# Graph message passing on one core: comparison constants in PSUM, picks on four banks in five turns, and 80 chunks moved from picks to gathers

## The chip, the core and the metric

The kernel runs on one core of a Trainium2 chip. Its five engines are named as the profile names them: PE (TensorE, with PEld for its weight loads), DVE (VectorE), ACT (ScalarE), POOL (GpSimd) and SP (SyncE, which only issues transfers here). The metric is the device time of one execution in microseconds, as the median of the runs. SBUF is the on-chip memory that all engines read; PSUM is the smaller one, in eight banks of 512 float32 columns by 128 partitions, into which PE writes its results.

## The reference, cut to what matters

`x` holds 12500 nodes of 128 numbers. There are 400000 edges, sorted by their target `dst`, with a random source `src` and a random type 0 or 1.

```python
Xs = X[src]
m_data = Xs @ W_data.T + b_data
m_ctrl = Xs @ W_control.T + b_control
msg = jnp.where((edge_types == 0)[:, None], m_data, m_ctrl)
agg = jax.ops.segment_sum(msg, dst, num_segments=X.shape[0])
out = jax.nn.relu(agg + (X @ W_self.T + b_self))
result = layernorm(x + out)
```

The kernel turns this round: it first sums the source rows of each target, apart for the two types, then multiplies the sums by the weights. So its bulk is a sum of 400000 rows of `x`, each row found by a random index. Every float32 row is kept as three bfloat16 parts (`x3` in SBUF, `rows3` in DRAM, 3 x 128 columns), so that products with zeros and ones keep the float32 value.

## The kernel before

**Chunks, groups, sets.** The edges make 3125 chunks of 128, in `NG` = 25 groups of `GC` = 125 chunks. A group is cut into five stretches of 25 chunks: 5 "p" chunks and 20 "e" chunks. What is done with the 20 e chunks of a stretch is called a set here (`pairs` in the code). The function `sets(g)` says for how many of the five stretches the e chunks are a set: five where `g % EACH == 0`, else four. In a group of four sets the last stretch's 20 e chunks are handled as p chunks too. With `EACH = 3` there are 109 sets and 945 p chunks.

**P chunks: gathers.** For each p chunk POOL issues one indirect transfer (`msg<-rows,idx_g`, in `fetch`), which brings the 128 source rows from DRAM. DVE compares near targets with a running number (`psel<-near_col,near`, one instruction for 25 chunks), which gives a matrix of zeros and ones, and PE adds the rows with three products of 48 columns (`sums<-psel,msg`, in `add_rows`). `paced` ties each gather to a product of PE (its gate), so that gathers are spread over a set; `due` says from when a gather may go out, some 14 chunks ahead of its use. The pool `msg` holds 18 rows' tiles.

**E chunks: picks.** The sources of a set (2560 edges) are sorted into 100 cells (`NCELL`), a cell for the 128 nodes of one block of `x3`, with up to 32 places (`CAP`) each; what finds no place goes through a spare gather (`both<-rows,idx`, one for two sets). A long chain on DVE finds the places: `O<-cell_col,blk` (which cell), the `prod` instructions (how many of the cell come before), `rm<-rank_col,rank`, `rv`, and last `pick`, a matrix of zeros and ones for the 3200 places. A product with `pick` as weights picks the rows out of `x3`: four cells make 128 rows in 384 columns, and 25 such quads (`NQ`) make a set, the last one with two cells of its own and two that the spare gather fills. These products are `got<-x,pick`, weights of 32 columns each, four of them side by side in the array's four column groups. ACT copies `got` out of PSUM as bfloat16 (`emsg<-got`), DVE makes the matrices of the targets (`esel<-code_col,code`, three instructions for a set, of 10, 9 and 6 quads) and PE adds the rows up (`sums<-esel,emsg`, 172 columns).

**Turns.** A set's picks are made in five turns of `unit(t)` in `picked`: 5, 5, 5, 4 and 5 quads, and in the fourth the half quad too. In a turn `rows` is called twice: two quads into the tile `got2` (two PSUM banks), the others into `got3` (three banks), each followed by one copy on ACT; then `add` adds the rows of the turn before. A quad's 384 columns leave 128 of its bank unused. The eight banks are: five for `got`, two for `sums`, one for `side` (small results). Each `got` tile has one buffer, so a turn's picks wait for the copy of the turn before.

**Comparisons.** All zero-and-one matrices but `pick` and the small ones come from `select` (line 541 before): a DVE comparison of a constant table in SBUF (`cell_col`, `rank_col`, `code_col`, `near_col`) with a tile of codes in SBUF, both bfloat16, where the table is read again for each chunk or cell.

**Order.** The order of work on each engine is written out: `merged` sorts the pieces of a set by a fraction of the set (`chunks`, `units`, `order`, `more`), and the engines run what they get in that order. While set w is picked, the chain of set w + 2 and the beginning of set w + 3 run on DVE. When a group's last sums are in, `pass_on` and `finish` carry its edge over and make the output rows; before the change this was tied to the end of the group's last p stretch.

## Time and profile before

| | |
|---|---|
| time, median of 3 runs | 1671.41 us (1670.22 to 1672.55) |
| the profiled execution | 1674.53 us |
| its span, first to last instruction | 1672.8 us |
| granted TensorE clock, mean | 0.992 |
| DVE busy | 1566.8 us, 94% |
| PE busy | 1542.5 us, 92% |
| POOL busy | 1244.2 us, 74% |
| ACT busy | 1221.0 us, 73% |

Busy time is the union of an engine's instructions. On DVE and PE an instruction's recorded time overlaps the next one's, so that sums over groups come out higher than busy time. POOL's rows are the issuing of gathers; the idle time between two gathers stands apart from the busy time. In the chain of waits the time is put on the engine that released each step.

### The profile page before, as it was taken

The page shows a single profiled execution, that of the slowest core. Times are in us where ns is not written, and L with a number is a line of the kernel's source. Part 1 is how long each engine was busy: PE and PEld are TensorE (multiplying, and loading weights), DVE is VectorE, ACT ScalarE, POOL GpSimd, SP SyncE. Part 2 cuts the span into 40 slices and gives each one's busy share as a digit, 9 for nine tenths or more (in the row PEclk, how much of TensorE's full clock was granted, in tenths as well). Part 3 has the DMA queues.
Part 4 walks back from the last instruction along what each step waited for, and adds up shares of the span by engine and source line. Part 5 has one row for each costly group of instructions (what it writes and reads, how often), then busy time and mean ns, then how long its engine had stood idle before and what let it go on. Part 6 is the DMA issues. An engine that isn't in the chain of part 4 may idle for free.

```text
span 1672.8 us, 67687 instructions
## 1 busy us (share of the span) xinstructions
PE 1542.5 (92%) x27966; PEld 1218.8 (73%) x27966; DVE 1566.8 (94%) x4078; ACT 1221.0 (73%) x2056; POOL 1244.2 (74%) x1022
## 2 busy tenths in 40 slices
PE   1699999999999999999999999999999999999988
PEld 0477777777777777777777777777777777777766
DVE  9799998999999999999999999999999999999983
ACT  7677776777777778667777778677777777777764
POOL 1377777767787787888787887878787787888881
PEclk9899999999999999999999999999999999999999
DMA  7944444554455454444454445454545444554541
GB/s 223 283 142 136 143 139 134 154 148 141 142 156 145 147 155 133 150 140 143 149 156 139 148 142 152 139 159 135 158 124 164 147 144 131 157 152 126 151 124 33
DMA packets 147605, 246.05 MB, mean 147 GB/s; under 512 B 35565, under 2 KB 114264, under 8 KB 147288
## 3 DMA queue, kind: packets, MB, share of 16 engines
q1 hardware_dynamic: 99128, 142.50, 25.4%
q0 software_dynamic: 48160, 99.14, 22.8%
q8 instruction: 221, 3.62, 0.9%
q14 instruction: 96, 0.79, 0.1%
HBM read 224.04 MB, written 17.52 MB: 144 GB/s over the span
## 4 chain that ended last, share of the span: by engine, by line
DVE 57%; PE 25%; issue 7%; ACT 6%; DMA 3%; DVEq 2%; SPq 0%; POOL 0%; ACTq 0%; POOLq 0%
PE sums L803 11%; DVE esel L541 8%; PE got L997 7%; DVE prod L656 5%; DVE prod L648 5%; DVE pick L790 5%; DVE O L541 4%; DVE rv L713 3%; DVE prod L627 3%; ACT emsg L1011 3%; PE side L1118 2%; DVE psel L541 2%; DVE found L666 2%; DVE rm L541 2%; DVE prod L612 2%
## 5 line engine op out<-in xcount | busy, mean ns | idle before, releaser
L887 POOL DMA_INDIRECT msg<-rows,idx_g x945 | 1174.7, 1243 | 302.4 <-issue 124.3
L1011 ACT CAST emsg<-got 128x768 bf16<-128x768 f32 x1090 | 964.5, 930 | 302.9 <-PE got L997 287.7
L803 PE MATMUL sums<-esel,emsg 128*128 128x172 bf16 x7848 | 693.1, 238 | 7.3 <-DVE acc L876 4.1
L803 PEld LDWEIGHTS <-emsg 128*128 128x128 bf16 x7848 | 570.8, 98 | 115.1 <-issue 104.2
L997 PE MATMUL got<-x,pick 128*32 128x384 bf16 x10682 | 561.7, 330 | 13.5 <-ACT emsg L1011 5.4
L997 PEld LDWEIGHTS <-pick 128*32 128x32 bf16 x10682 | 242.3, 96 | 140.0 <-issue 19.9
L541 DVE TENSOR_TENSOR esel<-code_col,code 128x1720 bf16<-128x1720 bf16 x327 | 292.8, 896 | 6.4 <-PE sums L803 6.3
L803 PE MATMUL sums<-psel,msg 128*128 128x48 bf16 x2835 | 162.6, 184 | 5.2 <-DVE acc L876 4.7
L803 PEld LDWEIGHTS <-msg 128*128 128x128 bf16 x2835 | 134.9, 97 | 14.1 <-issue 11.9
L656 DVE TENSOR_TENSOR prod<-prod 128x1200 bf16<-128x1200 bf16 x218 | 136.3, 625 | 5.5 <-DVE prod L648 1.2
L648 DVE TENSOR_TENSOR prod<-O,ahead 128x2000 bf16<-128x2000 bf16 x109 | 130.7, 1199 | 2.7
L541 DVE TENSOR_TENSOR O<-cell_col,blk 128x2000 bf16<-128x2000 bf16 x109 | 129.8, 1191 | 0.5 <-ACT blk L443 0.5
L963 POOL DMA_INDIRECT both<-rows,idx x55 | 64.4, 1171 | 70.0 <-DMA srcs<-in_src_dram 25.8
L726 PE MATMUL side<-rv,O 128*128 128x64 bf16 x2180 | 84.8, 195 | 32.9 <-DVE rv L713 32.0
L790 DVE TENSOR_SCALAR pick<-pick,lane_f 128x3200 bf16<-128x3200 bf16 x109 | 112.7, 1034 | 2.4 <-DMA pick<-there 2.4
L726 PEld LDWEIGHTS <-O 128*128 128x128 bf16 x2180 | 80.1, 100 | 43.0 <-DVE rv L713 24.8
L541 DVE TENSOR_TENSOR psel<-near_col,near 128x1200 bf16<-128x1200 bf16 x125 | 95.9, 767 | 0.0
L627 DVE TENSOR_TENSOR prod<-prod 128x500 bf16<-128x500 bf16 x327 | 94.3, 288 | 0.4
L713 DVE TENSOR_TENSOR rv<-rm,vals 128x1280 bf16<-128x1280 bf16 x109 | 89.4, 820 | 0.0
L622 DVE TENSOR_TENSOR prod<-O 128x1000 bf16<-128x1000 bf16 x109 | 73.9, 678 | 2.1 <-DVE bits L701 0.3
L876 DVE TENSOR_TENSOR acc<-acc,sums 128x172 f32 (+2 forms) x234 | 65.5, 280 | 6.3 <-PE sums L803 6.2
L642 DVE TENSOR_REDUCE ahead<-side 128x100 bf16<-128x200 f32 x109 | 39.2, 360 | 34.2 <-PE side L634 33.6
(197 smaller groups left out, 1522.4 us busy)
## 6 DMA issues: line engine op xcount, KB each, us to landing
pick<-there SPq DMA_DIRECT2D x108, 800.0 KB
msg<-rows,idx_g POOLq DMA_INDIRECT x945
acc<-acc_start SPq DMA_DIRECT2D x23, 640.0 KB
rows<-x SPq DMA_DIRECT2D x6, 1344.0 KB
xs<-in_x_dram SPq DMA_DIRECT2D x99, 62.5 KB
out_dram<-h SPq DMA_DIRECT2D x99, 62.5 KB
xt<-in_x_dram SPq DMA_DIRECT2D x6, 896.0 KB
cnt<-cnt_start SPq DMA_DIRECT2D x22, 160.0 KB
```

Source lines behind the costliest of these rows:

```text
L541: ins = nc.vector.tensor_tensor(sel.rearrange("p n (w t) -> p n w t", t=2), col[:rows].rearrange("p (o w t) -> p o w t", o=1, t=2).to_broa ...
L622: return nc.vector.tensor_add(h[:, :2 * CQ], s["O"][:, :2 * CQ], s["O"][:, 2 * CQ:])
L627: return nc.vector.tensor_add(h[:, to:to + n], h[:, a:a + n], h[:, b:b + n])
L648: return nc.vector.tensor_tensor(s["prod"][:, :, :NCELL], s["O"], s["ahead_b"].rearrange("p (o j) -> p o j", o=1).to_broadcast([P, EC, NCE ...
L656: return nc.vector.tensor_add(prod[:, :, :h], prod[:, :, :h], prod[:, :, h:2 * h])
L713: placed[:] = [nc.vector.tensor_tensor(rv.rearrange("p c v (r t) -> p c v r t", t=2), s["rm"].rearrange("p c (o r t) -> p c o r t", o=1, t ...
L726: nc.tensor.matmul(s["rk"][:m, :2 * CAP], s["held"][:, c * NCELL:c * NCELL + m], s["rv"][:, c].rearrange("p v r -> p (v r)"), start=(c == ...
L790: return nc.vector.tensor_scalar(t, t, lane_f, None, op0=OP.is_equal)
L803: last = nc.tensor.matmul(out, msg[:, j * D:(j + 1) * D], sel, start=(start and j == 0), stop=stop, skip_group_check=True)
L887: return nc.gpsimd.indirect_dma_start(out=msg, out_offset=None, in_=rows3[:, :], in_offset=bass.IndirectOffsetOnAxis(ap=codes["p", g][0][: ...
L997: last = behind(last, lambda: nc.tensor.matmul(ps[CAP * a:CAP * (a + 1), :], slots[w]["pick"][:, a * NQ + q, :], x3[:, 4 * q + a - a0].rea ...
L1011: s["out"] = nc.scalar.copy(msg[:, :n], ps[:, :n, :3 * D])
```

## The change

Three things are changed together.

**Constants in PSUM.** After the tables are built, `on_psum` copies each of them, two bfloat16 as one float32 word, into the tile `cols`, which takes one PSUM bank (250 of its 512 columns are used), and hands back a bfloat16 view of it. `select` is the same; its first input now lies in PSUM. This is five small copies at the start.

**Picks on four banks.** `got2` and `got3` become `got0` and `got1`, two banks each. The first two quads of a turn go to `got0`, the last two to `got1`. In a turn of five, the middle one is picked in its three parts of 128 columns, which go to the free ends of the banks: parts 0 and 1 in `got0`, part 2 in `got1`. So a quad of this kind is 12 products of 128 columns in place of 4 of 384. In the fourth turn the half quad is split in the same way. Over the kernel the picks go from 10682 products to 14070. ACT copies 1024 and 896 columns in place of 768 and 1152, and in the fourth turn the half quad takes two small copies in place of one.

**80 chunks.** `EACH` goes from 3 to 6: five groups in place of nine have five sets. So there are 105 sets and 1025 p chunks. To this belong: `paced` is called for a second gate in turns 1 and 3 (before: in turn 2), so 12 times a set; and the end of a group is now found as the later of its last p stretch and its last set (`ended`).

```diff
--- before.py
+++ after.py
@@ -32,7 +32,7 @@
 NE = 5
 NWIN = 2 * NE
 LAG = 2
-EACH = 3
+EACH = 6
 DPC = P * N // E
 PAD = 10
 PW = DPC + 2 * PAD
@@ -218,6 +218,7 @@
     ps1 = ctx.enter_context(tc.tile_pool(name="ps1", bufs=1, space=PSUM))
     ps2 = ctx.enter_context(tc.tile_pool(name="ps2", bufs=2, space=PSUM))
     psg = ctx.enter_context(tc.tile_pool(name="psg", bufs=1, space=PSUM))
+    psc = ctx.enter_context(tc.tile_pool(name="psc", bufs=1, space=PSUM))
 
     def side():
 
@@ -351,6 +352,18 @@
     rank_col = table(CAP, 0, "rank_col")
     code_col = table(2 * EW, 1, "code_col")
     near_col = table(2 * PW, 0, "near_col")
+    cols = psc.tile([P, 512], FP, name="cols")
+
+    def on_psum(t):
+        n = t.shape[1] // 2
+        at = cols[:, used[0]:used[0] + n]
+        used[0] += n
+        nc.vector.tensor_copy(at, t.bitcast(FP))
+        return at.bitcast(BF)
+
+    used = [0]
+    cell_cols = [on_psum(t) for t in cell_cols]
+    rank_col, code_col, near_col = on_psum(rank_col), on_psum(code_col), on_psum(near_col)
     ident_b = keep.tile([P, P], BF, name="ident_b")
     nc.vector.tensor_copy(ident_b, ident)
     lane_f = keep.tile([P, 1], FP, name="lane_f")
@@ -801,7 +814,7 @@
     def add_rows(out, msg, sel, start, stop):
         for j in range(3):
             last = nc.tensor.matmul(
-                out, msg[:, j * D:(j + 1) * D], sel, start=(start and j == 0), stop=stop, skip_group_check=True
+                out, msg[j], sel, start=(start and j == 0), stop=stop, skip_group_check=True
             )
         return last
 
@@ -940,7 +953,7 @@
             sel = s["sel"][:, c].rearrange("p (t w) -> p t w", t=2)
             at = DPC * c
             rows = cells_of(s["ps"], AW, 0).rearrange("p (t w) -> p t w", t=2)[:, :, at:at + PW]
-            add_rows(rows, s["msg"], sel, c == 0, c == n - 1)
+            add_rows(rows, [s["msg"][:, j * D:(j + 1) * D] for j in range(3)], sel, c == 0, c == n - 1)
             if c == 0:
                 counts.append(s)
             elif c == n - 1 and s in counts:
@@ -992,25 +1005,37 @@
             with after(first), tc.high_priority():
                 return f()
 
-        def pick(ps, q, a0=0, a1=4, last=None):
+        def pick(out, q, a0=0, a1=4, part=slice(None), last=None):
             for a in range(a0, a1):
                 last = behind(last, lambda: nc.tensor.matmul(
-                    ps[CAP * a:CAP * (a + 1), :], slots[w]["pick"][:, a * NQ + q, :],
-                    x3[:, 4 * q + a - a0].rearrange("p j d -> p (j d)"), start=True, stop=True, skip_group_check=True,
+                    out[CAP * a:CAP * (a + 1), :], slots[w]["pick"][:, a * NQ + q, :],
+                    x3[:, 4 * q + a - a0, part].rearrange("p j d -> p (j d)"),
+                    start=True, stop=True, skip_group_check=True,
                 ))
             return last
 
-        def rows(q, n, room, half=False):
-            ps = psg.tile([P, room, 512], FP, name=f"got{room}")
-            msg = two.tile([P, room, 3 * D], BF, name=f"emsg{room}")
-            for k in range(n):
-                last = pick(ps[:, k, :3 * D], q + k, last=last if k else None)
-                s["msg"][q + k] = msg[:, k, :]
+        def rows(q, n, k, half=False):
+
+            ps = psg.tile([P, 2, 512], FP, name=f"got{k}")
+            msg = two.tile([P, 2, 512], BF, name=f"emsg{k}")
+            shared = NQ - 1 if half else q + 2
+            first, last = (q, None) if k == 0 else (q + n - 2, None)
+            parts = (0, 1) if k == 0 else (2,)
+            for j in range(2):
+                last = pick(ps[:, j, :3 * D], first + j, last=last)
+                s["msg"][first + j] = [msg[:, j, d * D:(d + 1) * D] for d in range(3)]
+            for j, d in enumerate(parts):
+                ends = (lead, lead + 2) if half else (0, 4)
+                last = pick(ps[:, j, 3 * D:], shared, *ends, slice(d, d + 1), last)
+                if not half:
+                    s["msg"].setdefault(shared, []).append(msg[:, j, 3 * D:])
             if half:
-                last = pick(ps[:, n, :3 * D], NQ - 1, lead, lead + 2, last)
-            s["out"] = nc.scalar.copy(msg[:, :n], ps[:, :n, :3 * D])
-            if half:
-                nc.scalar.copy(s["msg"][NQ - 1][half_rows, :], ps[half_rows, n, :3 * D])
+                s["out"] = nc.scalar.copy(msg[:, :, :3 * D], ps[:, :, :3 * D])
+                to = s["last"][half_rows, parts[0] * D:(parts[-1] + 1) * D]
+                nc.scalar.copy(to.rearrange("p (k d) -> p k d", d=D), ps[half_rows, :len(parts), 3 * D:])
+            else:
+                width = 1024 if k == 0 else 512 + 3 * D
+                s["out"] = nc.scalar.copy(*(t.rearrange("p k d -> p (k d)")[:, :width] for t in (msg, ps)))
             return last
 
         def add(q0, q1):
@@ -1026,11 +1051,13 @@
                 assert not spare
                 if "both" in slots[w]:
                     slots[w]["last"] = two.tile([P, 3 * D], BF, name="last", bufs=1)
-                s["msg"][NQ - 1] = slots[w]["last"]
-            paced(w + (t + 0.5) / turns, rows(bounds[t], 2, 2))
+                s["last"] = slots[w]["last"]
+                s["msg"][NQ - 1] = [s["last"][:, d * D:(d + 1) * D] for d in range(3)]
+            n = bounds[t + 1] - bounds[t]
+            paced(w + (t + 0.5) / turns, rows(bounds[t], n, 0, t == 3))
             if t == 1 and w > 0 and w % 2 == 0:
                 spare.append(lambda: spare_rows(w))
-            gate = rows(bounds[t] + 2, bounds[t + 1] - bounds[t] - 2, 3, t == 3)
+            gate = rows(bounds[t], n, 1, t == 3)
             if t == 0:
                 choose(0, 10)
                 gates = ending() or [gate]
@@ -1044,7 +1071,7 @@
             if t > 0:
                 gates = add(bounds[t - 1], bounds[t])
             paced(w + (t + 1) / turns, gates[0])
-            if t == 2:
+            if t in (1, 3):
                 paced(w + (t + 1) / turns, gates[-1])
             for u in tiled.get(t, []):
                 u()
@@ -1237,6 +1264,10 @@
             due.append(at)
             n += 1
         closed.setdefault(int(at), []).append(p)
+    ended = {}
+    for g in range(NG):
+        last_p = next(w for w, ps in closed.items() if g * NE + NE - 1 in ps)
+        ended.setdefault(max(last_p, each_e.index((g, sets(g) - 1))), []).append(g)
 
     due[:] = [(LAG - 0.1) * (k + 0.5) / AHEAD for k in range(AHEAD)] + due[:-AHEAD]
 
@@ -1313,14 +1344,13 @@
         )
         slots.pop(w)
         rest = []
-        for p in closed.pop(w, []):
-            gp, ip = divmod(p, NE)
-            if ip == NE - 1:
-                rest.append(lambda gp=gp: pass_on(gp))
-                if gp < NG - 1:
-                    rest += finish(gp, range(4))
-                if gp + 2 < NG:
-                    rest.append(lambda gp=gp: begin_acc(gp + 2))
+        closed.pop(w, None)
+        for gp in ended.pop(w, []):
+            rest.append(lambda gp=gp: pass_on(gp))
+            if gp < NG - 1:
+                rest += finish(gp, range(4))
+            if gp + 2 < NG:
+                rest.append(lambda gp=gp: begin_acc(gp + 2))
     ending()
     for u in rest + last:
         u()
```

What the change does to the order of instructions is shown at three places.

DVE, the middle of the program, around the comparison for a set's last six quads (1032 columns; `prod`, `rm` and `rv` belong to the set two further on). Before:

```order
L656 TENSOR_TENSOR prod<-prod 128x20x60
L541 TENSOR_TENSOR esel<-code_col,code 128x1032
L656 TENSOR_TENSOR prod<-prod 128x20x30
L661 TENSOR_TENSOR prod<-prod 128x20x14
L666 TENSOR_REDUCE found<-prod 128x20
L612 TENSOR_TENSOR prod<-blk_21792,blk_184 128x20x20
L671 CAST rank<-found 128x40
L541 TENSOR_TENSOR rm<-rank_col,rank 128x640
L678 SCALAR_TENSOR_TENSOR key<-rank,pk 128x20
L541 TENSOR_TENSOR esel<-code_col,code 128x1720
```

and now:

```order
L669 TENSOR_TENSOR prod<-prod 128x20x60
L554 TENSOR_TENSOR esel<-cols,code 128x1032
L669 TENSOR_TENSOR prod<-prod 128x20x30
L674 TENSOR_TENSOR prod<-prod 128x20x14
L679 TENSOR_REDUCE found<-prod 128x20
L625 TENSOR_TENSOR prod<-blk_23265,blk_193 128x20x20
L684 CAST rank<-found 128x40
L554 TENSOR_TENSOR rm<-cols,rank 128x640
L691 SCALAR_TENSOR_TENSOR key<-rank,pk 128x20
L554 TENSOR_TENSOR psel<-cols,near_20978 128x1200
L726 TENSOR_TENSOR rv<-rm,vals_22769 128x1280
```

The instructions are the same, of the same shapes and nearly in the same order; what moved is that `esel`, `rm`, `psel` and `O` read `cols` in place of four tables.

POOL, the middle of the program; `both` is the spare gather that comes once in two sets. Before:

```order
L887 DMA msg<-rows_105,idx_g 128x384 x18
L963 DMA both<-rows_105,idx 128x384
L887 DMA msg<-rows_105,idx_g 128x384 x18
L963 DMA both<-rows_105,idx 128x384
L887 DMA msg<-rows_105,idx_g 128x384 x17
```

and now:

```order
L900 DMA msg<-rows_108,idx_g 128x384 x20
L976 DMA both<-rows_108,idx 128x384
L900 DMA msg<-rows_108,idx_g 128x384 x20
L976 DMA both<-rows_108,idx 128x384
L900 DMA msg<-rows_108,idx_g 128x384 x21
```

There were 17 or 18 gathers for two sets in this stretch, and now there are 20 or 21.

ACT, two turns of a set around the half quad (the fourth turn); 1024 and 896 or 768 and 1152 are columns. Before:

```order
L1011 CAST emsg_22288<-got_22287 128x768
L1011 CAST emsg_22301<-got_22300 128x1152
L1011 CAST emsg_22393<-got_22392 128x768
L1011 CAST emsg_22404<-got_22403 128x768
L1013 CAST last<-got_22403 64x384
L1011 CAST emsg_22469<-got_22468 128x768
L1011 CAST emsg_22482<-got_22481 128x1152
```

and now:

```order
L1038 CAST emsg_23359<-got_23358 128x1024
L1038 CAST emsg_23380<-got_23379 128x896
L1033 CAST emsg_23467<-got_23466 128x2x384
L1035 CAST both<-got_23466 64x256
L1033 CAST emsg_23485<-got_23484 128x2x384
L1035 CAST both<-got_23484 64x128
L1038 CAST emsg_23522<-got_23521 128x1024
L1038 CAST emsg_23543<-got_23542 128x896
```

The columns copied for a turn of five quads are 1920 as before, split otherwise, and the half quad has one more copy.

## The prediction

> **What bounds the kernel now.** I read the page's busy shares first, then the table of stretches, the chain, and the groups of POOL.
>
> ```profile
> PE 1542.5 (92%) x27966; PEld 1218.8 (73%) x27966; DVE 1566.8 (94%) x4078; ACT 1221.0 (73%) x2056; POOL 1244.2 (74%) x1022
> 800.00:1200.00 400.00, 383.56 (x7081) 306.43 (x7080) 385.39 (x981) 296.91 (x508) 318.35 (x260) 1.00 0.50 148
> DVE 57%; PE 25%; issue 7%; ACT 6%; DMA 3%; DVEq 2%; SPq 0%; POOL 0%; ACTq 0%; POOLq 0%
> L642 DVE TENSOR_REDUCE ahead<-side 128x100 bf16<-128x200 f32 x109 | 39.2, 360 | 34.2 <-PE side L634 33.6
> L726 PE MATMUL side<-rv,O 128*128 128x64 bf16 x2180 | 84.8, 195 | 32.9 <-DVE rv L713 32.0
> ```
>
> In 400 us of the middle DVE is busy for 385.39 and PE (first number) for 383.56: 96% both, at full clock. The chain runs on DVE for 57% and on PE for 25%, and the largest wait that DVE has for PE is 33.6 us in all, the largest of PE for DVE 32.0. So both are full, DVE a little more, and a cut counts only if both get it.
>
> POOL looks like the engine with room, at 74%. Its groups say otherwise:
>
> ```profile
> L887 POOL DMA_INDIRECT msg<-rows,idx_g x945 | 1174.7, 1243 | 302.4 <-issue 124.3 <-PE got L997 72.5 <-PE sums L803 64.0
> L963 POOL DMA_INDIRECT both<-rows,idx x55 | 64.4, 1171 | 70.0 <-DMA srcs<-in_src_dram 25.8 <-ACT emsg L1011 21.5 <-ACT idx L591 13.9
> L887 POOL DMA_INDIRECT msg<-rows,idx_g x945: 945/1122/4102, 66.8 to 1636.2; - x189
> ```
>
> A gather takes 1.243 us and 302.4 / 945 = 0.32 us stand before it, 1.563 together; 1000 gathers of both kinds make some 1560 us, and the first starts at 66.8, the last at 1636.2, 1569 us. POOL issues one gather behind the other all the time. It is full too, although nobody waits for it yet: the list of PE's waits has none for `msg`. And a gather can be as short as 0.945 us, so 0.298 us of the mean is something that holds it up. A stretch of POOL's and DVE's timelines shows what:
>
> ```profile
> 1041.27 0.94 POOL L887 DMA_INDIRECT msg<-rows,idx_g  x1 [0.30 <-issue]
> 1042.52 1.18 POOL L887 DMA_INDIRECT msg<-rows,idx_g  x1 [0.30 <-PE got L997]
> 1044.00 0.99 POOL L887 DMA_INDIRECT msg<-rows,idx_g  x1 [0.31 <-issue]
> ...
> 1041.17 0.39 DVE L876 TENSOR_TENSOR acc<-acc,sums 128x240 f32 x1
> 1041.48 0.25 DVE L627 TENSOR_TENSOR prod<-prod 128x200 bf16<-128x200 bf16 x1
> ...
> 1041.92 0.95 DVE L541 TENSOR_TENSOR esel<-code_col,code 128x1548 bf16<-128x1548 bf16 x1
> 1043.73 0.43 DVE L839 TENSOR_TENSOR acc<-acc 128x280 f32<-128x280 f32 x1
> ```
>
> The second gather starts inside `esel`, which ends at 1042.87, and the gather ends 0.83 us after that; the third starts inside line 839, which ends at 1044.16, and ends 0.83 us after that. Both DVE instructions read two tiles in SBUF. The first gather starts inside `acc<-acc,sums`, whose second input lies in PSUM, and is not held up. So a gather that begins under a DVE instruction with two SBUF inputs waits for that instruction's end, and one with an input in PSUM lets it pass.
>
> **The change part by part.** *Four sets fewer, on DVE.* The groups by shape, x109 once a set (busy us, mean ns):
>
> ```profile
> L648 DVE TENSOR_TENSOR prod<-O,ahead 128x2000 bf16<-128x2000 bf16 x109 | 130.7, 1199 | 2.7
> L541 DVE TENSOR_TENSOR O<-cell_col,blk 128x2000 bf16<-128x2000 bf16 x109 | 129.8, 1191 | 0.5 <-ACT blk L443 0.5
> L541 DVE TENSOR_TENSOR esel<-code_col,code 128x1720 bf16<-128x1720 bf16 x109 | 113.9, 1045 | 6.0 <-PE sums L803 5.9
> L790 DVE TENSOR_SCALAR pick<-pick,lane_f 128x3200 bf16<-128x3200 bf16 x109 | 112.7, 1034 | 2.4 <-DMA pick<-there 2.4
> L541 DVE TENSOR_TENSOR esel<-code_col,code 128x1548 bf16<-128x1548 bf16 x109 | 103.8, 953 | 0.4 <-PE sums L803 0.4
> L541 DVE TENSOR_TENSOR psel<-near_col,near 128x1200 bf16<-128x1200 bf16 x125 | 95.9, 767 | 0.0
> L713 DVE TENSOR_TENSOR rv<-rm,vals 128x1280 bf16<-128x1280 bf16 x109 | 89.4, 820 | 0.0
> L656 DVE TENSOR_TENSOR prod<-prod 128x1200 bf16<-128x1200 bf16 x109 | 85.6, 786 | 5.5 <-DVE prod L648 1.2 <-DVE acc L876 0.7
> L541 DVE TENSOR_TENSOR esel<-code_col,code 128x1032 bf16<-128x1032 bf16 x109 | 75.0, 688 | 0.0
> L622 DVE TENSOR_TENSOR prod<-O 128x1000 bf16<-128x1000 bf16 x109 | 73.9, 678 | 2.1 <-DVE bits L701 0.3 <-issue 0.3
> L541 DVE TENSOR_TENSOR rm<-rank_col,rank 128x640 bf16<-128x640 bf16 x109 | 53.2, 488 | 2.6
> L666 DVE TENSOR_REDUCE found<-prod 128x20 f32<-128x320 bf16 x109 | 52.2, 479 | 1.1
> ...
> L678 DVE SCALAR_TENSOR_TENSOR key<-rank,pk 128x20 f32<-128x20 bf16 x109 | 18.7, 171 | 0.0
> L876 DVE TENSOR_TENSOR acc<-acc,sums 128x172 f32 x109 | 35.3, 324 | 6.2 <-PE sums L803 6.2
> ```
>
> The large ones (without `psel`, which stays at 125) sum to 968 us, twelve smaller x109 groups from `found` 52.2 to `key` 18.7 to 402, and the spare slots' small ones to 71: 1441 / 109 = 13.2 us a set. Most records overlap the next by 0.08 us (in the timeline above 1041.17 + 0.39 against 1041.48), and a set has 26 of them: 13.2 - 2.1 = 11.1 us. Four sets: **-44 us on DVE**. The 80 chunks add nothing here, as `psel` already covers 25 chunks wherever it stands.
>
> *Four sets fewer and 80 chunks more, on PE.* From the chain in a stretch where PE leads (start, us, what):
>
> ```profile
> 828.07 0.93 PE got L997 x20
> 829.21 1.27 PE sums L803 x21
> 837.54 0.60 PE side L726 x20
> 838.14 0.15 PE sums L803 x6
> 855.25 0.26 PE sums L918 x12
> ```
>
> Six products of `msg` take 0.15 us, 0.025 each; 15 of `esel` the rest of 1.27, 0.075 each; 20 of `got` 0.93. A set has 98 of `got` (4.56 us), 72 + 3 of `esel` (5.6), 20 of line 726 (0.60) and about 0.6 us of small ones: 11.3, four sets -45 us. The chunks add 240 products of `msg`, +6 us. **-39 us on PE**.
>
> *The quad in three pieces.* No row has 128 columns on four column groups. Bounds: five quads of 384 columns take 0.93, 0.186 each; if 3 x 128 columns run as 384 do, the pieces cost nothing. `L918` is the nearest row, 12 products of 96 to 120 columns on two column groups in 0.26 us: six pairs, 0.043 a pair, 0.055 for 128 columns. If the pieces too ran only two at a time, 12 of them would take 6 x 0.055 = 0.33 in place of 0.186, +0.145 in each of four turns a set (in the half quad's turn two run side by side before and after): +61 us on PE over 105 sets. I take 0.01 a turn, +5 us, since `got` runs four groups side by side and `L918` shows that short products with loads between them keep their pace. PE then has -34.
>
> *ACT.* As many columns; one copy more a set:
>
> ```profile
> L1011 ACT CAST emsg<-got 128x768 bf16<-128x768 f32 x654 | 512.7, 802 | 300.5 <-PE got L997 286.5 <-ACT emsg L1011 3.7 <-PE sums L803 3.0
> L1011 ACT CAST emsg<-got 128x1152 bf16<-128x1152 f32 x436 | 489.6, 1123 | 2.4 <-PE got L997 1.3 <-PE side L747 0.2
> ```
>
> 384 columns more cost 0.32, so the fixed part of a copy is some 0.16 us: +17 us, in front of which ACT idles for 300 us waiting for PE. Hidden there; without that idle time it would cost those 17.
>
> *The constants: DVE's rate.* The 650 comparisons that are left (five a set, and 125 of `psel`) run at two elements a nanosecond now: from `rm` to `O`, 1360 columns cost 703 ns, 0.52 each, and 0.15 is fixed. No row has a two-byte input in PSUM. Float32 in PSUM is no dearer than in SBUF: line 839's group (both in SBUF) takes 0.43 for 280 in the rows above, `acc` with an input in PSUM 0.324 for 172, and between the two lie 1.0 ns a column. So the fixed part is the same, and the float32 pace is that of its type in both memories. Bounds: nothing, or one element a cycle as float32 has, +0.52 ns a column (the first rival). A gain I exclude, since it is POOL that waits for DVE and not DVE for POOL: an instruction with two SBUF inputs takes the same time whatever POOL does, as the spread of `rv` shows (shortest, median, longest):
>
> ```profile
> L713 DVE TENSOR_TENSOR rv<-rm,vals x109: 803/824/827, 28.2 to 1619.2; 128x1280 bf16<-128x1280 bf16 x109
> ```
>
> I take nothing. Five copies at the start, of few columns: +1.
>
> *The constants: POOL's time.* A gather that begins anywhere in an instruction of length L waits L/2 on average, so the delay goes with the sum of L squared over a set. The comparisons have `O` 1.42, `esel` 1.09 + 0.91 + 0.47, `rm` 0.24, `psel` 0.59 x 125/109: 4.8. What still holds the port has `prod` of `ahead` 1.44, `pick` 1.07, `rv` 0.67, 0.62, 0.46 and small ones 0.75: 5.0. So 0.298 goes to 0.15 and a gather to 1.10 us, bounds 0.945 and 1.243. There will be 1025 + 53 = 1078 gathers: 1078 x (1.10 + 0.32) = 1531, from 66.8, and behind the last one 1672.8 - 1636.2 = 37: POOL alone ends at 1635. With the 0.30 of the rows above in place of 0.32 it is 1613.
>
> *Sum.* Against the profiled execution's 1674.5: DVE -44, PE -34; weighted by their shares of the chain (57 and 25) -41, +1 for the start, +2 since POOL is as full as before: 1636.5. The profiled execution lies 3.1 above the median 1671.4; so 1633.
>
> **Rivals.** *One element a cycle (slower).* If a two-byte input in PSUM halves the rate, `O` grows by 1.04, `esel` by 2.24, `rm` by 0.33, 3.61 x 105 = 379, and `psel` by 0.62 x 125 = 78: 457 us on the engine that leads: 2090. It turns the sign from a tenth of that price on (41 us). For it: PSUM rows here all run at one a cycle. Against: they are all float32, and so does float32 in SBUF. [...]
>
> *POOL becomes the bound (slower).* If PSUM inputs of these comparisons held gathers up as before, 1078 x 1.563 + 104 = 1789, 1786 by the median. It decides from a mean gather of about 1.15 us, where POOL alone would end at the old time; the rows of 1041.27 speak against it.
>
> *Pieces two at a time (slower).* PE -39 + 61 = +22: 1693. It decides from some +35 on, where PE no longer gains.
>
> [...]
>
> *Twice the gain.* DVE and PE wait for one another for 33.6 and 32.0 us; with evenly sized `got` tiles and gathers that land earlier half of that may go: 1603.
>
> **Chances.** Forecast 0.66, one element a cycle 0.10, POOL 0.06, pieces 0.04, dearer start 0.05, twice the gain 0.09. The likeliest one's own range is 1612 to 1655: PE's -34 alone or less at the top, DVE's whole -44 and some waits at the bottom. Extended to the twice-gain and the no-change case it is 1602 to 1673, which leaves 0.20 out, all of it above. About 0.2% (3 us) is what can be told from no change. Faster: 0.66 + 0.09 = 0.75. Same: 0.05. Slower: 0.20.
>
> **What would show it.** `O<-cols` at 1.19 us and `esel` at 0.69 to 1.05, as now: no loss of rate; at 2.2 us the first rival. Gathers' mean near 1.10, with many of 0.945 that begin under `esel` or `O`: the port is free; idle time before them over 0.30 says that POOL now waits for its gates. 28 products of `got` in 0.95 us or so: pieces run four wide. DVE's busy time falls to some 1523 and PE's to 1508, each still 96% of the middle. Wrong I am if the time falls much less while both busy times fall as said: then POOL's gathers are late, and PE has waits for `msg`.

## The result, and the profile after

The changed kernel took 1648.41 us (median of 4 runs, 1645.56 to 1649.66), the kernel before on the same chip 1670.82 us (1670.08 to 1672.55): a ratio of 0.9865, with a 95% interval from 0.9852 to 0.9877. That is 22.4 us less, where 38 were forecast. The profiled execution took 1648.49 us; the forecast for it was 1636.5. One thing is needed to read the times further down: beside the runs whose labels begin with e, f and h the kernel before takes 1948 to 1983 us in place of 1671, and in the traces of these runs PE halts without a recorded reason.

The changed kernel's page (first its span, then the busy times, then the chain), and one row of its table of stretches:

```profile
span 1646.4 us, 74069 instructions
PE 1514.0 (92%) x31152; PEld 1247.6 (76%) x31152; DVE 1542.1 (94%) x3979; ACT 1200.0 (73%) x2097; POOL 1157.8 (70%) x1100
DVE 53%; PE 28%; issue 8%; ACT 7%; DMA 2%; DVEq 2%; POOL 0%; SPq 0%; ACTq 0%; POOLq 0%
500.00:900.00 400.00, 383.71 (x7971) 319.34 (x7969) 386.29 (x995) 296.60 (x526) 303.07 (x281) 1.00 0.52 153
```

DVE is busy for 24.7 us less than before, PE for 28.5 us less, and both still fill 96% of the middle. The gain is there, and it is smaller on both engines than said. DVE's groups by shape:

```profile
L554 DVE TENSOR_TENSOR O<-cols,blk 128x2000 bf16<-128x2000 bf16 x105 | 125.0, 1190 | 0.5 <-ACT blk L456 0.5
L554 DVE TENSOR_TENSOR esel<-cols,code 128x1720 bf16<-128x1720 bf16 x105 | 109.0, 1038 | 0.9 <-PE sums L816 0.9
L554 DVE TENSOR_TENSOR psel<-cols,near 128x1200 bf16<-128x1200 bf16 x125 | 96.0, 768 | 0.3 <-issue 0.3
L554 DVE TENSOR_TENSOR rm<-cols,rank 128x640 bf16<-128x640 bf16 x105 | 51.5, 490 | 3.3
L679 DVE TENSOR_REDUCE found<-prod 128x20 f32<-128x320 bf16 x105 | 50.8, 484 | 3.1
L684 DVE CAST rank<-found 128x40 bf16<-128x40 f32 x105 | 28.7, 274 | 0.0
```

The five comparisons cost what they cost from SBUF (`O` 1190 ns against 1191, `esel` 1038 against 1045). One row has become dearer, and the change doesn't touch it: `rank`, a copy of 40 columns from SBUF to SBUF, takes 274 ns. It took 180 before:

```profile
L671 DVE CAST rank<-found 128x40 bf16<-128x40 f32 x109 | 19.7, 180 | 0.0
```

POOL's groups, and the spread of the gathers (shortest, median, longest, then the first and the last start):

```profile
L900 POOL DMA_INDIRECT msg<-rows,idx_g x1025 | 1091.4, 1065 | 360.7 <-issue 142.6 <-PE got L1010 95.5 <-PE sums L816 83.4
L900 POOL DMA_INDIRECT msg<-rows,idx_g x1025: 940/946/2039, 68.9 to 1613.6; - x171
```

The median gather is now one that nothing holds up, 946 ns where it was 1122, and the idle time before a gather is 0.35 us where it was 0.32: POOL now waits for its gates. ACT's copies take 1012 and 911 ns, together as much as the 802 and 1123 before, behind an idle time for PE's picks:

```profile
L1038 ACT CAST emsg<-got 128x1024 bf16<-128x1024 f32 x420 | 425.0, 1012 | 176.6 <-PE got L1010 160.9 <-issue 3.1 <-ACT both L1035 2.5
L1038 ACT CAST emsg<-got 128x896 bf16<-128x896 f32 x420 | 382.6, 911 | 14.0 <-PE got L1010 13.0 <-PE side L760 0.3 <-issue 0.2
```

And the picks of two turns of five quads, in the chain of a stretch where PE leads:

```profile
849.27 0.93 PE got L1010 x28
851.74 0.93 PE got L1010 x28
```

28 products, 16 of 384 columns and 12 of 128, take the 0.93 us that 20 of 384 took.

**Where DVE's missing 20 us are.** Two things were found in the two traces. The first is `rank`. The rows of POOL and DVE around one of them (start, us, then what):

```profile
1058.82 0.95 POOL L900 DMA_INDIRECT msg<-rows,idx_g  x1 [0.30 <-issue]
...
1058.62 0.49 DVE L679 TENSOR_REDUCE found<-prod 128x20 f32<-128x320 bf16 x1
1059.14 0.38 DVE L625 TENSOR_TENSOR prod<-blk,blk 128x400 bf16<-128x400 bf16 x1
1059.44 0.34 DVE L684 CAST rank<-found 128x40 bf16<-128x40 f32 x1
1059.81 0.49 DVE L554 TENSOR_TENSOR rm<-cols,rank 128x640 bf16<-128x640 bf16 x1
```

The gather runs from 1058.82 to 1059.77. `rank` starts inside it and ends at 1059.78, with the gather's end. The `prod` of line 625, which starts 0.3 us earlier, isn't held. In 89 of the 105 sets `rank` starts during a gather. In 63 of them it starts 0.53 to 0.77 us into one, that is in its last 0.2 to 0.4 us, and ends with it; in the other 26 it takes at most 191 ns. In all it costs 9.8 us more than 105 copies of 180 ns would. Before the change `rank` started during a gather too, in 74 of 109 sets, but ended with one in only 3: what changed is the point of the gather at which it starts.

The second is the order. The scheduler placed `esel` (1720 columns) between `found` and the `prod` that `found` needs in 43 of 109 sets before, and in none of 105 now; `found` stood right behind that `prod` in 33 sets and stands there in 91 now. In both traces an instruction that needs the result of the one right before it starts 34 ns after its end; one that doesn't starts some 83 ns ahead of it. Counted over all of DVE's records, gaps of 30 to 40 ns went from 467 to 561 (562 in g_after, the same kernel again). Each costs 0.117 us, of which the 0.083 of lost overlap shows in DVE's busy time: 94 of them are 11 us, 8 of it busy time.

### The profile page after: what moved, and what is told of

Its sections match the earlier page's. It is cut to its first block, busy times and chain, and to the rows that moved or that the text cites. A ratio compares the mean times of both kernels' runs of the same rounds, so it can differ in the third digit from the quotient of the medians.

```text
span 1646.4 us, 74069 instructions
## 1 busy us (share of the span) xinstructions
PE 1514.0 (92%) x31152; PEld 1247.6 (76%) x31152; DVE 1542.1 (94%) x3979; ACT 1200.0 (73%) x2097; POOL 1157.8 (70%) x1100
## 4 chain that ended last, share of the span: by engine, by line
DVE 53%; PE 28%; issue 8%; ACT 7%; DMA 2%; DVEq 2%; POOL 0%; SPq 0%; ACTq 0%; POOLq 0%
PE sums L816 12%; PE got L1010 8%; DVE esel L554 7%; DVE prod L669 5%; DVE prod L661 5%; DVE O L554 4%; DVE pick L803 4%; PE side L1145 3%; DVE prod L640 3%; DVE rv L726 3%; DVE prod L635 3%; DVE rm L554 2%; DVE found L679 2%; ACT emsg L1038 2%; DVE prod L625 2%
## 5 line engine op out<-in xcount | busy, mean ns | idle before, releaser
L900 POOL DMA_INDIRECT msg<-rows,idx_g x1025 | 1091.4, 1065 | 360.7 <-issue 142.6
L1038 ACT CAST emsg<-got 128x1024 bf16<-128x1024 f32 x840 | 770.9, 961 | 190.6 <-PE got L1010 173.9
L1010 PE MATMUL got<-x,pick 128*32 128x384 bf16 (+1 forms) x14070 | 553.4, 286 | 10.5 <-ACT emsg L1038 3.4
L554 DVE TENSOR_TENSOR esel<-cols,code 128x1720 bf16<-128x1720 bf16 (+2 forms) x315 | 280.7, 892 | 0.9 <-PE sums L816 0.9
L1033 ACT CAST emsg<-got 128x768 bf16<-128x768 f32 x210 | 168.4, 802 | 126.7 <-PE got L1010 119.1
L554 DVE TENSOR_TENSOR O<-cols,blk 128x2000 bf16<-128x2000 bf16 x105 | 125.0, 1190 | 0.5 <-ACT blk L456 0.5
L739 PE MATMUL side<-rv,O 128*128 128x64 bf16 (+1 forms) x2100 | 82.0, 195 | 27.3 <-DVE rv L726 26.4
L739 PEld LDWEIGHTS <-O 128*128 128x128 bf16 (+1 forms) x2100 | 76.6, 100 | 30.5 <-DVE rv L726 26.6
L554 DVE TENSOR_TENSOR psel<-cols,near 128x1200 bf16<-128x1200 bf16 x125 | 96.0, 768 | 0.3 <-issue 0.3
L640 DVE TENSOR_TENSOR prod<-prod 128x500 bf16<-128x500 bf16 (+2 forms) x315 | 89.8, 285 | 0.6
```

The costliest lines, as they stand in the source:

```text
L554: ins = nc.vector.tensor_tensor(sel.rearrange("p n (w t) -> p n w t", t=2), col[:rows].rearrange("p (o w t) -> p o w t", o=1, t=2).to_broa ...
L640: return nc.vector.tensor_add(h[:, to:to + n], h[:, a:a + n], h[:, b:b + n])
L739: nc.tensor.matmul(s["rk"][:m, :2 * CAP], s["held"][:, c * NCELL:c * NCELL + m], s["rv"][:, c].rearrange("p v r -> p (v r)"), start=(c == ...
L900: return nc.gpsimd.indirect_dma_start(out=msg, out_offset=None, in_=rows3[:, :], in_offset=bass.IndirectOffsetOnAxis(ap=codes["p", g][0][: ...
L1010: last = behind(last, lambda: nc.tensor.matmul(out[CAP * a:CAP * (a + 1), :], slots[w]["pick"][:, a * NQ + q, :], x3[:, 4 * q + a - a0, pa ...
L1033: s["out"] = nc.scalar.copy(msg[:, :, :3 * D], ps[:, :, :3 * D])
```

## The experiments

There are four edits of the changed kernel: constants back in SBUF, `EACH = 3`, `rank` by an addition, and an earlier `esel`. The first two and the last two are also combined. Some edits were run more than once, and so have two or three labels. "A chip on which PE halts" is a short name: whether it is the chip or its state at the time isn't shown (the record numbers the chip 1 for the e runs and for the g runs alike).

| edit | label, on a chip like the first | labels on chips where PE halts |
|---|---|---|
| none | g_after | |
| constants in SBUF | g_sbuf | e1_sbuf, f1_sbuf |
| `EACH = 3` (109 sets) | g_each3 | e2_each3 |
| both of these, so that only the picks' turns are new | | e3_picks, h_picks |
| `rank` by an addition from PSUM | | e4_rank, h_rank |
| `esel` for the first ten quads earlier | | f5_first |
| these last two together | g_both | |

### The first six runs: chips on which PE halts

Constants in SBUF (e1_sbuf, f1_sbuf):

```diff
-    cell_cols = [on_psum(t) for t in cell_cols]
-    rank_col, code_col, near_col = on_psum(rank_col), on_psum(code_col), on_psum(near_col)
```

> The changed kernel with its constants back in SBUF (picks on four banks and 105 sets stay). If the comparisons' place is what frees gathers, a gather goes back from 1.065 to about 1.2 us, nearly all of them behind one another with 0.305 between: 1078 x 1.5 + 104 = 1720, up to 1770, with PE or DVE waiting for msg or POOL idle at 0.305 throughout. Rival: POOL's room does not matter and the constants only changed the order of DVE's instructions, in which esel of 1720 columns stands before found again here: then 1630 to 1645, a little faster than the changed kernel.

109 sets (e2_each3), and 109 sets with constants in SBUF, that is the diff above and this one (e3_picks):

```diff
-EACH = 6
+EACH = 3
```

> The changed kernel with EACH = 3: 109 sets and 945 gathers as before, constants in PSUM, picks on four banks. If the shortfall of the gain sits in DVE's set (rank held up by gathers, 0.09 us, and found, same and rm standing right behind what they need, 0.12 us a set), this kernel is slower than the one before by 109 x 0.2 = 22 us: about 1690. If it sits in the 80 chunks (more gathers, more work for PE), this is the kernel before, 1671, or a little faster.

> The picks on four banks alone: EACH = 3 and constants in SBUF. Products in pieces cost nothing: 1671 to 1676, and 28 products of got in 0.93 us as 20 before. Rival: the smaller room of got (four banks) and the twelfth copy on ACT cost some 0.1 us a turn: 1700 or more.

`rank` written by an addition of a zero in PSUM (e4_rank); it is the same number:

```diff
+    nil = cols[:, 500:501]
+    nc.vector.memset(nil, 0.0)
...
-                return nc.vector.tensor_copy(
-                    s["rank"], s["found"].rearrange("p (c o) -> p c o", o=1).to_broadcast([P, EC, 2])
+                return nc.vector.tensor_add(
+                    s["rank"], s["found"].rearrange("p (c o) -> p c o", o=1).to_broadcast([P, EC, 2]),
+                    nil.rearrange("p (c o) -> p c o", o=1).to_broadcast([P, EC, 2]),
```

> The changed kernel, but rank is written by an addition whose second input is a zero in PSUM, in place of a copy from SBUF to SBUF. If the copy is held by gathers (0.274 us in place of 0.180), the addition takes about 0.19 us at any time, 105 x 0.09 = 9 us off DVE's chain: 1638 to 1642. If rank's length only fills a wait that another link of the chain would have, the time stays at 1648.

The `esel` for the first ten quads of the next set put into the written order, between `eighth` and `found` (f5_first):

```diff
...
+            (0.515, (lambda prev: choose_early(w + 1, prev)) if w + 1 < pairs else None),
...
-                choose(0, 10)
+                if w == 0:
+                    choose(0, 10)
+                else:
+                    for k in range(10):
+                        s["sel"][k] = early_sel[w][:, k]
```

> The changed kernel, but with the comparison of a set's first ten quads (esel, 1720 columns) written into the order of the set before it, between the last halving of prod and found, where it stood in 43 of 109 sets before the change and in none after. If the shortfall lies in DVE's order (an instruction right behind the one it needs starts 0.12 us later than one with other work between), this gives back 0.12 us in some 90 sets, 11 us: 1636 to 1640 where the changed kernel has 1648, and found's wait behind prod (0.034 us of idle time each) is gone. Rival: the place of esel is no cause, the time stays at 1648, or grows because esel now waits for PE to free its buffer.

> The changed kernel with its constants back in SBUF (picks on four banks and 105 sets stay), on a chip on which PE isn't halted. If the comparisons' place is what frees gathers: a mean gather of 1.2 us or more, nearly all 0.305 us behind one another, and 1078 x 1.5 + 104 = 1720, up to 1770. Rival: POOL's room does not matter: 1630 to 1648, since esel of 1720 columns stands before found again here.

Measured, each beside the kernel before on its chip:

| label | sets | us | before, us | ratio and interval |
|---|---|---|---|---|
| e1_sbuf | 105 | 2024.67 | 1948.16 | 1.0381 (1.0325 to 1.0436) |
| e2_each3 | 109 | 1960.00 | 1948.16 | 1.0049 (1.0022 to 1.0076) |
| e3_picks | 109 | 1962.12 | 1948.16 | 1.0069 (1.0039 to 1.0099) |
| e4_rank | 105 | 2012.49 | 1948.16 | 1.0320 (1.0261 to 1.0378) |
| f5_first | 105 | 2052.20 | 1982.77 | 1.0363 (1.0324 to 1.0402) |
| f1_sbuf | 105 | 2048.71 | 1982.77 | 1.0338 (1.0294 to 1.0383) |

The kernel before takes 17 to 19% longer here than on the first chip (no trace of it was kept here), so a time that an expectation gives for a chip like the first is not tested by these. What sets the end here is in e2_each3's page, the busy times and, of POOL's groups, the gathers:

```profile
PE 1674.1 (85%) x31890; PEld 1339.7 (68%) x31890; DVE 1598.5 (81%) x4083; ACT 1235.6 (63%) x2165; POOL 1050.1 (53%) x1022
L900 POOL DMA_INDIRECT msg<-rows,idx_g x945 | 973.2, 1030 | 733.5 <-PE got L1010 319.4 <-PE sums L816 262.4 <-issue 81.6
```

PE alone leads; POOL idles 582 us for PE's gates and DVE has 19% to spare, so room on DVE and POOL can't show. The weight loads' waits of e4_rank (in all, times, longest) show PE standing still with nothing to wait for:

```profile
PEld L1013 <- issue: 262.8, 565, 1.6
```

I counted the places at which two instructions of PE or its weight loads start over 0.33 us apart though neither waits for anything:

```
                     sets   such gaps   us in all
before, first chip    109        0          0
changed, first chip   105        0          0
e2_each3, e3_picks    109   221, 245    127, 135
e4_rank, f5_first     105   323, 334    187, 192
e1_sbuf, f1_sbuf      105   364, 384    202, 222
```

So kernels with 105 sets have 1.3 to 1.7 times the halts of those with 109, 52 to 95 us more, which is about the size of what they are slower by (e4_rank and e1_sbuf 52 and 63 us above e2_each3 and e3_picks). The counted gaps are not all of the difference, though: e2_each3 is 268 us above g_each3, the same kernel on a chip like the first, and its gaps sum to 127; e1_sbuf is 265 us above g_sbuf and has 202. Why kernels with 105 sets halt more is open, and so is what halts PE at all.

What can still be read is the gathers' mean, and it follows the place of the constants whatever the number of sets: 1.176 us (e1_sbuf), 1.163 (f1_sbuf) and 1.191 (e3_picks) with constants in SBUF, 1.030 (e2_each3) and 1.028 (e4_rank) in PSUM. And `rank` by addition takes 187 ns in e4_rank, where as a copy it takes 210 in e2_each3.

### The parts apart, on a chip like the first

The expectations from here on describe `EACH = 6` and `EACH = 3` as "six picks to an eviction" and "three sections' picks in a turn", which is wrong: what differs is how many groups have a fifth set, 105 or 109 sets in all. Their numbers of sets, chunks and gathers are the right ones.

> The changed kernel again, nothing altered, as the measure for the three others of this call. Theory: the change is worth its 1.3 per cent only where PE runs without the halts that the traces of the first experiments show (gaps of about 0.57 us with no wait, 221 to 384 of them, none in the two traces of the first chip). Where the kernel before takes about 1671 us, this one takes 1645 to 1652 (ratio 0.987) and its trace has no such gaps. Where the kernel before takes 1900 us or more, PE alone bounds, and this one takes 3 to 4 per cent longer than the one before (ratio 1.03 to 1.04), with over 300 such gaps, as the three other kernels with six picks to an eviction did there. Rival: those three were slow by what they altered (constants back in SBUF, rank by an addition, esel earlier); then the ratio is 0.99 to 1.01 on such a chip too.

> The changed kernel with the constants of the comparisons back in SBUF. Theory that the constants' place counts by the gathers: a gather's mean goes from 1.065 us to about 1.18 (as the two earlier runs with constants in SBUF show), 1025 of them make 118 us more for POOL, which then sets the end again: 1650 to 1675 us where the kernel before takes 1671, some 0.3 to 1.5 per cent above the changed kernel. Rival: the constants' place is worth nothing for the end, since DVE and PE bound; then the time is that of the changed kernel within 0.3 per cent, or some 8 to 15 us below, because esel stands before found again in about half of the sets and rank (274 ns) goes back to 180 to 195 ns. On a chip that halts PE: as the changed kernel within 1 per cent by both.

> The changed kernel with rank written by an addition of zero from PSUM, and with the first ten chunks' esel of the next set put between eighth and found. Theory that DVE's missing 20 us are the rank held by gathers and the bare dependencies: rank's mean goes from 274 to about 190 ns (8.8 us over 105), found's start is covered by esel (5 to 10 us less), DVE's busy time falls from 1542 to 1523 to 1530 us, and the time, on a chip where the kernel before takes 1671 us, from 1648 to 1630 to 1640. Rival: PE, at 92 per cent, bounds just as well; then DVE's busy time falls so, and the time stays at 1645 to 1650. On a chip that halts PE: as the changed kernel within 1 per cent by both.

> The changed kernel with three sections' picks instead of six in a turn: 109 sets instead of 105, the 80 chunks back from the gathers to the picks; constants stay in PSUM. Theory that the moved chunks relieve DVE and PE: four more sets at the changed kernel's busy time to a set (1542 over 105 is 14.7 us of DVE for everything, 11.1 for the set's own instructions) are 40 to 45 us of DVE and 30 to 39 of PE, so 1670 to 1690 us where the kernel before takes 1671, that is all of the gain or more is gone. Rival: the gain comes from the gathers made shorter by the constants in PSUM, and the number of sets counts little: 1640 to 1655 us. On a chip that halts PE: 2 to 4 per cent below the changed kernel, as in the first run of it.

The kernel before took 1670.16 us (1667.65 to 1673.53) here.

| label | us | ratio and interval | DVE busy | PE busy | gather, us | `rank`, ns |
|---|---|---|---|---|---|---|
| g_after | 1647.00 | 0.9869 (0.9852 to 0.9885) | 1541.3 | 1514.6 | 1.062 | 264 |
| g_sbuf | 1759.69 | 1.0532 (1.0515 to 1.0550) | 1533.2 | 1544.5 | 1.232 | 185 |
| g_each3 | 1692.48 | 1.0128 (1.0105 to 1.0152) | 1586.6 | 1548.3 | 1.054 | 263 |
| g_both | 1644.69 | 0.9852 (0.9836 to 0.9868) | 1525.5 | 1519.8 | 1.076 | 187 |

**g_after** repeats the first result. It doesn't decide why the kernels with 105 sets were slow on the other chips, since this chip doesn't halt PE (no such gap in its trace).

**g_sbuf**: my theory named the sign, and its 1650 to 1675 is far too low. A `msg` gather is not 1.18 but 1.232 us, nearly the 1.243 of the kernel before, and with the spare ones there are 1078. Its POOL rows, and the largest waits of ACT and PE that follow from them:

```profile
L898 POOL DMA_INDIRECT msg<-rows,idx_g x1025 | 1262.8, 1232 | 318.1 <-issue 131.7 <-PE sums L814 63.8 <-PE got L1008 56.7
L898 POOL DMA_INDIRECT msg<-rows,idx_g x1025: 942/1120/5209, 67.6 to 1727.1; - x171
...
ACT last L1080 <- DMA both<-rows,idx: 112.2, 29, 9.5
...
PE sums L814 <- ACT last L1080: 73.5, 19, 8.0
...
DVE acc L887 <- PE sums L814: 68.0, 18, 7.7
```

From 67.6 to 1727.1 POOL issues 1078 gathers of both kinds, 1.54 us each with the gap before it. It is late, and who feels it first is the spare gather: it is queued behind the `msg` gathers on POOL, ACT's copy `last` waits for its rows (112.2 us, up to 9.5 at once), PE's sums wait for ACT, and DVE's `acc` for PE. In the kernel before ACT's wait for the same rows was

```profile
ACT last L1055 <- DMA both<-rows,idx: 12.7, 6, 6.2
```

and in the changed kernel no such wait is among ACT's larger ones. So the rival that POOL stays the bound, priced at 1786 us in the prediction, is what happens without the constants in PSUM, 26 us below that price. The expectation of e1_sbuf and f1_sbuf, 1720 and up to 1770 on such a chip, is met here. The 1.18 that I had used for the expectation came from the chips that halt PE, where POOL idles longer (608.4 and 640.6 us before 1025 gathers in e1_sbuf and f1_sbuf, 318.1 here); it doesn't carry over.

**g_each3** took 1692, as the expectation of e2_each3 had it (about 1690), a little above the theory's 1670 to 1690 and far from the rival's 1640 to 1655. Against g_after it has four sets more and 80 gathers fewer: DVE 45.3 us more, PE 33.7 more. Against the kernel before it has the constants in PSUM and the new turns, with as many sets: DVE 19.8 us more, PE 5.8 more, and 22 us more in time. `esel` stands right before `found` in none of its 109 sets, as in the changed kernel, in 50 of 105 in g_sbuf and in 57 of 109 in e3_picks: so it is the constants in PSUM that move it. With 945 gathers POOL has nothing to gain from shorter ones:

```profile
PE 1548.3 (92%) x31890; PEld 1281.7 (76%) x31890; DVE 1586.6 (94%) x4083; ACT 1243.8 (74%) x2165; POOL 1071.5 (63%) x1022
L900 POOL DMA_INDIRECT msg<-rows,idx_g x945 | 995.9, 1054 | 453.0 <-PE got L1010 183.2 <-PE sums L816 123.0 <-issue 114.9
```

So the parts of the change, by time against the kernel before; the other three have the new turns:

| | 109 sets | 105 sets |
|---|---|---|
| constants in SBUF | 0 (the kernel before, old turns) | +90 us |
| constants in PSUM | +22 us | -23 us |

With the new turns, the constants in PSUM without the 80 chunks and the 80 chunks without the constants each make the kernel slower than it was; what the turns alone do on such a chip isn't shown. Shorter gathers are worth nothing while POOL isn't asked for more of them, and more gathers can't be had while each takes 1.54 us.

**g_both** gives DVE back most of what it had lost. Its groups, and the spread of `rank` there and in g_after:

```profile
L556 DVE TENSOR_TENSOR esel<-cols,code 128x1720 bf16<-128x1720 bf16 x105 | 109.8, 1046 | 14.5 <-PE sums L819 13.7 <-issue 0.4
L681 DVE TENSOR_REDUCE found<-prod 128x20 f32<-128x320 bf16 x105 | 49.8, 474 | 0.0
L686 DVE TENSOR_TENSOR rank<-found,cols 128x40 bf16<-128x40 f32 x105 | 19.6, 187 | 0.0
L686 DVE TENSOR_TENSOR rank<-found,cols x105: 176/188/197, 26.4 to 1589.6; 128x40 bf16<-128x40 f32 x105
```

```profile
L684 DVE CAST rank<-found x105: 167/273/409, 26.4 to 1595.2; 128x40 bf16<-128x40 f32 x105
```

`rank` now never takes over 197 ns, `found` stands right behind its `prod` in one set only (91 in g_after), and gaps of 30 to 40 ns fall from 562 to 455. DVE's busy time falls by 15.8 us, as the theory said (1523 to 1530). The time falls by 2.3 us, within what the two intervals can't tell apart, and above the 1630 to 1640 of the theory. The rival is nearer: PE bounds as well. The rows of the middle and the chain say so:

```profile
DVE 41%; PE 40%; ACT 8%; issue 6%; DMA 3%; DVEq 1%; SPq 0%; ACTq 0%
500.00:900.00 400.00, 387.23 (x7960) 317.59 (x7961) 381.10 (x995) 295.20 (x523) 295.20 (x280) 1.00 0.50 152
```

PE is at 96.8% and DVE at 95.3%, and `esel` in its new place waits 13.7 us for PE's sums. So the two causes account for 16 of DVE's 20 us, and they account for next to nothing of the time.

### The last two

> The picks on four banks alone: three sections' picks in a turn as before (109 sets, 945 gathers), constants in SBUF as before, only the turns and the products in pieces as in the changed kernel. The kernel with the constants in PSUM besides and 109 sets took 1692 us where the one before takes 1670, with DVE busy 1586.6 us (20 more than before) and PE 1548.3 (6 more). Theory: the 20 us on DVE are the constants' (rank held by gathers, bare dependencies by the new order), the 6 us on PE the pieces'. Then this kernel has DVE at 1563 to 1570 us, rank at 180 to 195 ns, PE at 1546 to 1550 and takes 1668 to 1680 us. Rival: the new turns of the picks cost DVE the 20 us; then DVE's busy time is 1580 to 1590 and the time 1685 to 1695 us.

> The changed kernel with rank alone written by an addition of zero from PSUM; esel stays where it is. With both alterations DVE's busy time fell by 16 us and the time only from 1647.0 to 1644.7 us, while PE's busy share rose from 92 to 93 per cent and esel waited 14.5 us for PE's sums. Theory that PE bounds as closely as DVE does: rank falls to about 187 ns, DVE's busy time by 8 to 10 us to 1532 to 1535, and the time is 1643 to 1648 us where the kernel before takes 1670. Rival: the earlier esel gives back by its waits for PE what rank's addition gains; then rank's addition alone is worth its 9 us, and the time is 1636 to 1641 us.

Again a chip that halts PE; the kernel before took 1949.85 us. h_picks took 1963.69 (ratio 1.0065, 1.0041 to 1.0089) with 241 halts, h_rank 2019.50 (1.0341, 1.0304 to 1.0377) with 334. Neither time answers its question. `rank`'s means, 197 ns as a copy with constants in SBUF and 187 as an addition, are near what was said (180 to 195, and about 187).

What these traces do show is DVE's order, whose counts are nearly the same on both kinds of chip: gaps of 30 to 40 ns number 579 in g_each3 and 581 in e2_each3, 497 in g_sbuf and 503 and 504 in e1_sbuf and f1_sbuf. With the new turns alone, in 109 sets, they are 537 (h_picks) and 539 (e3_picks), where the kernel before has 467, and the constants in PSUM bring them to 579. So of 112 more gaps about 70 come with the new turns and 42 with the constants, and what the constants move is mostly at `found` (33 before, 28 with the turns alone, 89 in g_each3).

So two things stay untested on the first kind of chip: the new turns alone, and the addition alone. And since h_rank, which differs from the changed kernel in one small instruction a set, is 3.4% slower than the kernel before there, the gain found here must be taken as that of chips like the first; the changed kernel itself wasn't run on one that halts PE.

No version beats the changed kernel by more than can be told: g_both's 1644.69 is the lowest median seen.

## Why the prediction was right or wrong

*DVE and PE both full, and POOL full behind them.* Right. g_both shows that a cut for DVE alone buys 2 us for 16, g_sbuf that POOL without shorter gathers ends 90 us later.

*Four sets fewer on DVE, -44.* Right for what it counts: 45.3 us between g_each3 and g_after. The forecast for DVE failed elsewhere, in the step on the constants' rate, "A gain I exclude, since it is POOL that waits for DVE and not DVE for POOL", and "I take nothing". The term that was missing is +20 us on DVE (19.8 between the kernel before and g_each3). About half of it is `rank`, 28.7 us in g_each3 against 19.7. I had tested the claim on one instruction, `rv`, whose time doesn't depend on POOL (803 to 827 ns before). It is false for `rank`: gathers that are no longer held up start and end at other points of DVE's work, and in 63 of 105 sets the copy now starts near the end of one and is held till it ends; before it was 3 of 109, and in g_sbuf, with the constants back in SBUF, it is 4 of 105.

The other half is order, 112 more bare dependencies in g_each3, 9 us of busy time at 0.083 each. The listings of DVE's order in the section on the change show the 1720-column `esel` gone from its stretch, and I read past it. This half doesn't belong to the constants alone: by the counts under "The last two" about 70 of the 112 come with the new turns, for which the prediction had a term on PE and one on ACT and none on DVE. That split is counted, not timed, since the turns weren't run alone on this kind of chip. g_both, which removes the held copies and most of the gaps at `found`, gives back 16 of the 20 us of busy time.

*Four sets fewer and 80 chunks more on PE, -39; the pieces, +5.* The mechanism is right and the first size off: -33.7 and +5.8 by busy time, so -28.5 (1514.0 against 1542.5) where -34 was forecast. The pieces cost nothing that shows: 28 products take 0.93 us as 20 did, where two at a time were estimated at 0.145 more, so I take it that they run four wide.

*ACT hidden; the constants' rate.* Right. The two copies of a turn sum to 1923 ns against 1925, behind 177 us of idle time. A comparison of two-byte numbers with one input in PSUM keeps its two elements a nanosecond: from `rm` (640 columns, 490 ns) to `O` (2000, 1190 ns) a column costs 0.51 ns, where it was 0.52 from SBUF. So the rival at 2090 is out, with its one element in 1.0 ns, and so is the dearer start of a PSUM read, to which 0.05 was given: `O` takes 1190 ns from PSUM and 1191 from SBUF, `rm` 490 and 488.

*POOL's time.* Right, and so was the sign of its idle time (0.35 us before a gather, 0.32 before). A gather takes 1.065 us where 1.10 was said. Of 390 gathers that start under `esel`, `psel` or `O`, 389 take at most 0.96 us; before, 13 of 388 did. What the prediction calls the port is known from these times alone; what a gather waits for in the hardware isn't shown. POOL's last one starts at 1613.6, some 16 us later than the sum has it (1635 less the 37 behind it).

*The sum.* "DVE -44, PE -34; weighted by their shares of the chain" gave -41. With the measured cuts, -24.7 and -28.5, the span fell by 26.4, between the two, as any such weights would have it. Weights, though, are the wrong tool for cuts of different sizes: g_both's DVE was 41 us below the kernel before and its PE 23, and the median moved by 25.5, near the smaller cut. So even with DVE's -44 in full, some -28 would have been the better sum, by PE. The missing 20 us on DVE therefore explain little of the 15 us by which the time lies above the forecast: the 16 of them that g_both gives back bring 2.3. That PE's cut sets the time is read from g_both alone.

The measured 1648.41 us lies in the prediction's own narrower range of 1612 to 1655, near its upper end, for which it had given "PE's -34 alone or less".

## What to carry to other kernels

When two engines are both at 96%, as here, forecast a change by the smaller of their two cuts (g_both: 41 and 23 us of busy time, 25.5 of the median), and look for the third engine that the change asks more of before counting either. Shortening what a queue issues and giving that queue more to issue can be worth nothing apart and something only together (here, with the new turns, +22 and +90 us apart, -23 together). When a change lets two engines overlap that took turns before, list the short instructions that now fall beside the other engine's work (here `rank`, 180 to 274 ns), and compare the written order with the order that the scheduler made of it, row by row.

## What the runs showed of the hardware

DVE and POOL hold each other up in both directions, and which way depends on the instruction. A gather that starts under a DVE instruction with two SBUF inputs waits for its end, and mostly ends 0.82 us after that (before the change, under `esel`, `psel` and `O`, 337 of 388 end 0.81 to 0.84 us after it); under a comparison with one input in PSUM it takes 0.946 us (median; 389 of 390 at most 0.96). Two inputs of full size aren't needed for it: under `pick`, one tensor with one number for each partition, none of 68 gathers took less than 0.96 us (median 1.70), while under the reduction `found`, with its one SBUF input, 67 of 68 did. In turn DVE's copy of 40 columns from SBUF to SBUF, float32 to bfloat16, that starts 0.53 to 0.77 us into a gather of 0.946 lasts till the gather's end (up to 423 ns in place of some 176). A bfloat16 product from SBUF that starts 0.3 us into the gather is not held in the rows shown, and an addition with one input in PSUM in the copy's place stays at 176 to 197 ns in g_both; in h_rank 22 such additions start 0.6 to 0.7 us into a gather, and none is held.

In the traces of the e, f and h runs two starts on PE lie about 0.57 us apart with no wait between them, 221 to 384 times an execution, at weight loads and products alike; the granted clock there is 0.963 to 0.979, but g_sbuf has 0.965 with no such gap. A kernel takes 15 to 19% longer there, more than these gaps sum to, and 105 sets in place of 109 are then slower (e1_sbuf 63 us above e3_picks) where on a chip like the first they are faster (g_after 45 us below g_each3). What it is was not found.
